# Preparing the weights of a two-layer attention block: order of loads, sums of squares, a third quantised tile

## The chip, the cores and the metric

One core of one Trainium2 chip. The metric is device time in microseconds (us): the median of three runs of the kernel before, 2736.28 (2727.44 to 2742.57). The program has five engines with queues of their own: TensorE (PE), VectorE (DVE), ScalarE (ACT), GpSimd (POOL) and SyncE (SP), which issues all the DMAs here.

## The reference

All arithmetic is fp32, x is [8, 512, 256]. Two layers, each adding two branches of the same normalised input to x:

```
xn = layernorm(x)
L0: q,k,v = split(xn @ Wq.T), split(xn @ Wk.T), split(xn @ Wv.T)   # 16 heads of 64
    k, v  = concat(mem_k, k), concat(mem_v, v)                     # 64 memory keys per head
    dots  = mix(q @ k * scale, pre_proj)                           # heads mixed: "bhij,hk->bkij"
    dots  = causal mask; keep each row's 64 largest; softmax
    out   = (mix(attn, post_proj) @ v) @ Wout.T + bout
    ffn   = fp4(silu(fp4(xn) @ fp4(w_gate).T) * (fp4(xn) @ fp4(w_up).T)) @ fp4(w_down).T
    x     = x + out + ffn
xn = layernorm(x)
L1: u = silu(xn @ Wg + bg) * (xn @ Wi + bi);  y = Cp * causal_conv(u, Bp * A^t) + Dp * u
    y = norm(y) * gamma + beta
    y = (silu(y @ Wfg + bfg) * (y @ Wfu + bfu) @ Wfd + bfd) @ Wo + bo
    lin = xn @ int4(kernel) + bias + (xn @ a) @ b
    x = x + y + lin
```

`fp4` scales blocks of 16 columns by their largest magnitude, rounds to eight levels and scales back; `int4` does it with one scale for the whole matrix, from its largest magnitude.

## The kernel before

The kernel has a preparation (to about 110 us of the profile), the attention of the eight batches (to about 2115 us), and a last stage with L0's feed-forward and L1. Only the preparation is touched; it makes from the weights what the other two need.

**Folded attention weights.** Wq, Wk and pre_proj are folded into one matrix per mixed head, `mg` (and `mgm` for the memory keys). A loop over 20 groups `j` of 16 key columns does this: PE multiplies a block-diagonal copy of Wk (`bd`, made by DVE and ACT) with Wq into a PSUM bank `pa` (8 instructions of 32 rows per group; an fp32 product leaves two records); the bank is copied to an SBUF tile `both`, by ACT for even `j` and by DVE for odd `j`; PE multiplies it with the mixing matrix `kr` into a bank `pm` (4 instructions of 256 columns); ACT copies that to `mg` or `mgm`. Groups 16 to 19 are the memory keys. Two banks serve `pa`, three `pm`, three all transposes. For a first guess at each row's 64th largest score the kernel needs the mean squares of the folded weights: after each group ACT squares `pm` into a `junk` tile (two of them, used in turn), and DVE adds up its groups of 16 (L781 and L782); at the end they are summed over `j` (L784, L785) and over partitions by a product with `ones` (L789), giving `tot`.

**L0's feed-forward weights.** `prepare` (L369 to L518) quantises w_gate and w_up in six blocks of 128 rows and 512 columns (the last has 64 rows), then w_down in two of 704 columns. A block runs through `fp4_steps` (L325): DVE takes the largest magnitudes (`w_amax`), scale and reciprocal; POOL multiplies; ACT takes `Abs` and `Sign`; six DVE steps round in `w_hi`, `w_lo` and `w_a`; POOL multiplies `w_lo` by the signs and by the scales. PE then transposes `w_lo`, and DVE or ACT copies the result from PSUM. Source, `w_a`, `w_lo` and `w_hi` have two copies, `quantise` takes them in turn.

**L1's weights** are collected in one tile, `w1s`, of 8 KB in each partition: Wfg and Wfu with gamma folded in (DVE), the int4 matrix plus a @ b (DVE, from a PSUM bank), and Wfd @ Wo (ACT). Scaling of the int4 matrix needs its largest magnitude over all partitions: DVE reduces to `mx`, POOL reduces over partitions to `mxa`, DVE computes `s` and `r` from it. When all are there, one DMA stores `w1s` to DRAM (`w1_d`). Wv, Wout and the first batch's normed tokens are transposed by PE and copied by ACT in between.

**What sets the order.** Each instruction of the preparation is recorded by `Straight` (L169) with its readers and writers, and `Plan.run` (L118) writes a fixed order for PE, ACT, DVE and POOL. It simulates: each instruction has an estimated cost (L196 to L221) and a due time, the length of what depends on it plus a lateness (`r.late`). A DMA is an SP operation of 0.5, then an operation on a shared `wire` of bytes / 240e3, then 2.0 of waiting (L252 to L259). SP's instructions are placed by the framework, not by this plan. On the chip each engine takes its instructions strictly in that order, so an instruction that waits holds all behind it. Each SP issue also waits for the DMA that used its semaphore eight issues earlier.

After the preparation, tiles of new pools take the space of its tiles, and may be written when the last reader of that space, DMAs included, is done. The first of them are the value tile `v` (ACT, L942) and `rows` (POOL, L962, a copy of the normed tokens), which PE needs for the products L975 and L1004. The pools `scr` and `x2p` (tile `xnT`) have two buffers each. Batch 0's tokens hold the first `scr` during the preparation, the next batch's tokens are loaded to the second (L883) and normed by DVE at L290 to L306, in whose queue `first_guesses` (L521), twelve or so small DVE operations around one ACT `Tanh`, six times over, stands before and after.

Of the kernel before, what the change touches and what calls it, by code (L numbers as in the profile page):

```python
# [20 lines left out]
HC = H * DH // P  # L21
MEM = 64
# [32 lines left out]
FI = 704  # L55
# [113 lines left out]
class Straight:  # L169
# [4 lines left out]

    def __init__(self, nc, pl):
        self.nc, self.pl, self.seen, self.run, self.late = nc, pl, {}, None, 0.0

# [3 lines left out]
    class Engine:  # L181
# [3 lines left out]
        def __getattr__(self, what):  # L185
            return lambda *a, **k: self.owner.call(self.name, what, a, k)

    @staticmethod
# [7 lines left out]
    @staticmethod  # L196
    def cost(eng, what, out, ins, k):
        n = 1
        for d in out.shape[1:]:
            n *= d  # L200
        wide = n
        for t in ins:
            m = 1
            for d in t.shape[1:]:
                m *= d
            if eng != "PE":
                wide = max(wide, m)
        if eng == "PE":
            if what == "transpose":
                return 0.05 + 0.0007 * n  # L210

            return (0.04 + 0.00175 * n) * (0.35 if out.shape[0] == 32 else 1.0)
        if eng == "DVE":
            if what == "tensor_tensor_scan":
                return 0.2 + 0.0021 * n
            return 0.17 if wide < 48 else 0.13 + (0.0007 if what == "tensor_scalar" else 0.00105) * wide
        if eng == "ACT":
            return 0.22 + 0.00083 * wide + {AF.Sqrt: 1.3, AF.Tanh: 1.3, AF.Silu: 0.4}.get(k.get("func"), 0.0)
        if eng == "POOL":
            return 6.0 if what == "partition_all_reduce" else 0.15 + 0.0005 * wide if what == "memset" else 0.35 + 0.0018 * wide  # L220
        return 0.5  # L221

    def call(self, name, what, a, k):
# [7 lines left out]
        func = {"func": next((t for n, t in aps if n == "func"), None)} if eng == "ACT" else {}  # L231
        cost = self.cost(eng, what, out, ins, func)
        deps = []
        for t, write in [(t, False) for t in ins] + [(t, True) for t in outs]:
# [17 lines left out]
        if what == "dma_start":  # L252
            size = 4.0
            for d in out.shape:
                size *= d
            done = self.pl.add("wire", size / 240e3, lambda: None, [op])
            done.late = self.late
            done = self.pl.add(f"wait{id(op)}", 2.0, lambda: None, [done])
            done.late = self.late  # L259
# [108 lines left out]

def prepare(nc, a, pw, scratch, ident, vt, cb, wgu_d, wd_d, w1_d, bsum_d, spare, place):  # L369

# [22 lines left out]
    for i in range(2):  # L393
        q = {"src": pw.tile([P, FI], F32, name=f"w_v{i}")}
        q["v"] = q["src"]
        for k in ("a", "lo", "hi"):
            q[k] = pw.tile([P, FI], F32, name=f"w_{k}{i}")
        for k in ("amax", "scale", "rec"):
            q[k] = pw.tile([P, FI // BLK], F32, name=f"w_{k}{i}")
        sets.append(q)  # L400

    def quantise(i, m, n, loads):
        q = {k: t[:m, : n // BLK if k in ("amax", "scale", "rec") else n] for k, t in sets[i].items()}
        for cols, src in loads:
            nc.sync.dma_start(q["src"][:, cols], src)
        for _, _, step in fp4_steps(nc, q, m, n):
            step()
        return q["lo"]

    for i, r in enumerate(range(0, FI, P)):  # L410
        m = min(P, FI - r)
        q = quantise(i % 2, m, 2 * D, [
            (slice(u * D, (u + 1) * D), a[f"L0_ffn_{n}"][r : r + m, :]) for u, n in enumerate(("w_gate", "w_up"))
        ])
# [11 lines left out]
    for o in range(DC):  # L426
        q = quantise(o, P, FI, [(slice(0, FI), a["L0_ffn_w_down"][o * P : (o + 1) * P, :])])
        for c0 in range(0, FKC, 3):
# [9 lines left out]

    w1s = pw.tile([P, 4, DC, D], F32, name="w1s")
    w1 = {i + 2: w1s[:, i] for i in range(4)}  # L440
    for i, n in enumerate(("Wg", "Wi")):
# [69 lines left out]
    for c in range(DC):  # L511
# [5 lines left out]
        nc.vector.tensor_tensor(w1[4][:, c, :], ps[:, :D], w4[:, c, :], ALU.add)  # L517
    nc.sync.dma_start(w1_d[:, 2 * DC * D :], w1s.rearrange("p i c f -> p (i c f)"))  # L518

# [81 lines left out]
def block_kernel(ctx: ExitStack, tc: tile.TileContext, a: dict, out: bass.AP):  # L601
# [48 lines left out]
    with ExitStack() as c0:  # L650
# [30 lines left out]
        with tc.tile_pool(name="prep", bufs=1) as prep, tc.tile_pool(name="prep_ps", bufs=1, space=PSUM) as pps:  # L681
            pl = Plan({})
            r = Straight(nc, pl)
            banks = [pps.tile([P, 512], F32, name=f"pps{i}") for i in range(8)]
# [23 lines left out]
            xn = scr.tile([P, NT * D], F32, name="scr").rearrange("p (t d) -> p t d", d=D)  # L708
            r.sync.dma_start(xn, x_in[0])
            por = prep.tile([P, H], F32, name="por")  # L710
            r.sync.dma_start(por, a["L0_attn_post_proj"].unsqueeze(1).to_broadcast([H, RB, H]))
# [31 lines left out]
            both = [prep.tile([P, 512], F32, name=f"both{i}") for i in range(3)]  # L743
            junk = [prep.tile([P, 512], F32, name="junk"), ring[:, 11776:]]
            sqp = prep.tile([P, NJ, DC * H], F32, name="sqp")
            for j in range(NJ):
# [33 lines left out]
                r.scalar.copy(dst, pm.rearrange("p (e k i) -> p e k i", e=DC, i=16))  # L780
                r.scalar.activation(junk[j % 2], pm, AF.Square)  # L781
                r.vector.tensor_reduce(sqp[:, j], junk[j % 2].rearrange("p (q i) -> p q i", i=16), AX.X, ALU.add)  # L782
            sq = prep.tile([P, 2, DC * H], F32, name="sq")
            r.vector.tensor_reduce(sq[:, 0], sqp[:, :16].rearrange("p j q -> p q j"), AX.X, ALU.add)  # L784
            r.vector.tensor_reduce(sq[:, 1], sqp[:, 16:].rearrange("p j q -> p q j"), AX.X, ALU.add)  # L785
            ones = prep.tile([P, P], F32, name="ones")
            r.gpsimd.memset(ones, 1.0)
            ps = bank("a")
            r.tensor.matmul(ps[:, : 2 * DC * H], ones, sq.rearrange("p i q -> p (i q)"), start=True, stop=True)  # L789
            r.vector.tensor_copy(tot.rearrange("p i e k -> p (i e k)"), ps[:, : 2 * DC * H])  # L790
# [63 lines left out]
            r.late = 0.0  # L854
            prepare(r, a, prep, lambda: bank("t"), ident, vt, cb, wgu_d, wd_d, w1_d, bsum_d, wv, ring[:, 8192 : 8192 + DC * 2 * FI])
            r.late = 1000.0
# [1034 lines left out]
```

## Time and profile before the change

| | |
|---|---|
| median of the runs | 2736.28 us |
| profiled execution, its own time | 2738.95 us |
| its span | 2737.0 us |
| preparation to PE's first L933 | 110.1 us |
| mean granted PE clock, whole span | 0.953 |
| clock 0 to 110 us | 0.89 |

The span covers the engines' work of one execution; its own time has some 2 us around it. The profile names all recorded preparation instructions by one line, the recorder's call, L239 (L248 in the changed program); they are told apart by tile. Busy time of an engine in a stretch counts its instructions' durations; a matmul of fp32 leaves two records. In a list of waits a line reads: engine and tile that waited, engine or DMA it waited for, total, number, longest. In a timeline a line's bracket is the idle time before it and the releaser.

### The profile page before, as it was taken

Reading aid. Unit: us, or ns where it says so; the run is one execution under the profiler, and the core shown is the slowest. Engines: PE = TensorE matmul, PEld = TensorE weight load, DVE = VectorE, ACT = ScalarE, POOL = GpSimd, SP = SyncE. Lnnn points to the kernel's source line nnn. Section 1 sums busy time; section 2 is a strip of 40 time slices with the busy share of each in tenths; the row PEclk is TensorE's granted clock in tenths of the full one; section 3 lists DMA queues with packets and bytes.
Section 4 is the critical chain, followed back from the end, with each engine's and each line's share of the span. In section 5 each row is a group of like instructions: output and inputs, shape, how many; then the busy total and the mean of one; then the engine's idle time right before and its main releaser. Section 6 shows DMA issues by size and latency. Waiting matters only on the chain. (4 is left out here: it accounts for less than half of the span.)

```text
span 2737.0 us, 56067 instructions
## 1 busy us (share of the span) xinstructions
PE 2516.0 (92%) x19064; PEld 1943.5 (71%) x19064; DVE 2181.5 (80%) x7022; ACT 1908.1 (70%) x5332; POOL 1058.7 (39%) x2175
## 2 busy tenths in 40 slices
PE   7899999999999999999999999999966688999997
PEld 4677877887787688778777877877755555666664
DVE  7788888798779779877987887797889688877762
ACT  4468877778797788778878977877795345544342
POOL 3203433444343434434443443344333354444330
PEclk9899999999999999999999999999988789999998
DMA  4300100100010010001000100000100021000000
GB/s 140 153 25 18 36 20 11 36 20 21 18 28 22 17 36 21 21 18 30 20 19 21 36 19 20 21 19 21 56 20 7 30 88 31 24 16 16 8 8 16
DMA packets 114859, 82.61 MB, mean 30 GB/s; under 512 B 79339, under 2 KB 108806, under 8 KB 113798
## 3 DMA queue, kind: packets, MB, share of 16 engines
q1 hardware_dynamic: 114566, 78.95, 9.6%
q8 instruction: 153, 2.51, 0.4%
q14 instruction: 140, 1.15, 0.1%
HBM read 44.04 MB, written 35.39 MB: 29 GB/s over the span
## 5 line engine op out<-in xcount | busy, mean ns | idle before, releaser
L1087 ACT ACTIVATE junk<-ring,cur 128x96 int8<-128x96 f32 (+36 forms) x1288 | 743.4, 585 | 3.7 <-POOL cur L1122 3.7
L1091 DVE TENSOR_SCALAR_CACHE_REDUCE junk<-ring,cur 128x520 int8<-128x520 f32 (+29 forms) x1208 | 574.5, 517 | 60.1 <-POOL cur L1149 58.7
L1044 PE MATMUL ps_sc<-xnT,tk 128*128 128x8 f32 (+38 forms) x2048 | 534.6, 401 | 11.9 <-ACT ring L1050 11.7
L1004 PE MATMUL ps_mi<-rows,mg 128*128 128x128 f32 x4096 | 509.1, 280 | 12.3 <-ACT scr L981 9.2
L1004 PEld LDWEIGHTS ps_mi<-rows,mg 128*128 128x128 f32 x4096 | 488.0, 194 | 43.9 <-issue 16.6
L1044 PEld LDWEIGHTS ps_sc<-xnT,tk 128*128 128x128 f32 x2048 | 338.5, 193 | 144.6 <-issue 76.5
L1186 DVE SCALAR_TENSOR_TENSOR ring<-ring,kth,e 128x520 f32<-128x520 f32 (+56 forms) x512 | 281.8, 570 | 186.2 <-ACT e L1177 181.0
L1322 PE MATMUL ps_at<-mixd,ring 128*128 128x128 f32 x2560 | 341.0, 282 | 13.3 <-POOL mixd L1279 12.5
L1322 PEld LDWEIGHTS ps_at<-mixd,ring 128*128 128x128 f32 x2560 | 314.0, 194 | 51.9 <-issue 21.3
L1157 DVE SCALAR_TENSOR_TENSOR y<-ring,cur 128x520 f32<-128x520 f32 (+56 forms) x512 | 297.5, 581 | 9.5
L1050 ACT COPY ring<-ps_sc 128x456 f32<-128x456 f32 (+56 forms) x512 | 190.4, 380 | 153.5 <-PE ps_sc L1044 151.6
L1160 DVE MAX8 top<-y 128x8 f32<-128x520 f32 (+56 forms) x512 | 255.7, 499 | 17.6
L1087 ACT ACTIVATION_READ_ACCUMULATOR junk<-ring,cur 128x1 f32 x1288 | 255.7, 198 | 0.0
L1346 PEld LDWEIGHTS ps_y<-at,v 128*64 128x64 f32 (+1 forms) x6144 | 199.3, 140 | 64.9 <-ACT at L1328 19.4
L1177 ACT ACTIVATE e<-ring 128x520 f32<-128x520 f32 (+56 forms) x512 | 229.5, 474 | 22.4 <-DVE ring L1186 21.7
L1015 ACT COPY tk<-ps_mi 128x256 f32<-128x256 f32 x512 | 172.4, 379 | 104.1 <-PE ps_mi L1004 102.1
L1103 POOL TENSOR_TENSOR cur<-base,raw 128x8 f32<-128x8 f32 x153 | 38.9, 254 | 524.6 <-ACT junk L1087 517.1
L1346 PE MATMUL ps_y<-at,v 128*64 128x64 f32 (+1 forms) x6144 | 225.0, 227 | 17.8 <-ACT at L1328 12.2
L1328 ACT COPY at<-ps_at 128x512 f32<-128x512 f32 x320 | 185.7, 583 | 74.6 <-PE ps_at L1322 73.9
L1139 POOL TENSOR_TENSOR by<-gap,minus 128x8 f32<-128x8 f32 x120 | 205.4, 1712 | 9.4
L1279 POOL TENSOR_TENSOR mixd<-mix,rden 128x512 f32<-128x512 f32 x128 | 132.4, 1054 | 105.6 <-DVE rden L1271 93.4
L239 PE MATMUL ps_gu<-mg,ring 128*128 128x352 f32 x448 | 148.9, 478 | 15.2 <-DVE hid L239 10.3
(324 smaller groups left out, 3881.7 us busy)
## 6 DMA issues: line engine op xcount, KB each, us to landing
msd<-scr SPq DMA_DIRECT2D x32, 512.0 KB
ring<-msd SPq DMA_DIRECT2D x512, 32.0 KB
scr<-in_L_attn_x_dram SPq DMA_DIRECT2D x10, 512.0 KB
mg_d<-mg SPq DMA_DIRECT2D x1, 4096.0 KB
att<-o SPq DMA_DIRECT2D x64, 64.0 KB
ring<-in_L_attn_x_dram SPq DMA_DIRECT2D x8, 512.0 KB
ring<-att SPq DMA_DIRECT2D x8, 512.0 KB
out_dram<-ring SPq DMA_DIRECT2D x8, 512.0 KB
```

Source lines behind the costliest of these rows:

```text
L1004: nc.tensor.matmul(ps[:, j * P : (j + 1) * P], mg[:, e, k + j, e2 * P : (e2 + 1) * P], toks(e), start=(e == 0), stop=(e == DC - 1),)
L1044: nc.tensor.matmul(ps[:, :ntok], q["tk"][side_of(g)][e][:, b].rearrange("p k i -> p (k i)"), o["xnT"][:, e, :ntok], start=(e == 0), stop=( ...
L1050: nc.scalar.copy(s[:, b, MEM : MEM + ntok], q.pop(("ps", b))[:, :ntok])
L1087: nc.scalar.activation(junk, src, AF.Sign, bias=thr, scale=-1.0, accum_out=raw[:, b : b + 1])
L1091: nc.vector.tensor_scalar(junk, src, thr, 0.0, ALU.is_ge, ALU.add, accum_out=raw[:, b : b + 1])
L1139: eng.tensor_tensor(by, gap[:, 1], minus, ALU.pow)
L1157: nc.vector.scalar_tensor_tensor(y, src, cur[:, 0, b : b + 1], src, ALU.is_ge, ALU.subtract, reverse1=True)
L1160: nc.vector.max(out=top[:, b, 1:], in_=y)
L1177: nc.scalar.activation(e, src, AF.Exp, scale=1.0 / SMALL)
L1186: nc.vector.scalar_tensor_tensor(src, src, kth[:, b : b + 1], e, ALU.is_ge, ALU.mult, accum_out=den[:, b : b + 1])
L1322: nc.tensor.matmul(pt[:n, b * P : (b + 1) * P], s[:, 4 * j + b, col : col + n], w["mix"][j][:, b, :], start=True, stop=True,)
L1346: nc.tensor.matmul(w["py"][j * DH : (j + 1) * DH, q * GR : (q + 1) * GR], vs[c][:n, k * DH : (k + 1) * DH], ats[c][:n, k, :], start=(c == ...
```

## The change

Six things, all in the preparation:

- The sums of squares of groups 0 to 15 are taken from the finished `mg`: after groups 7 and 15, sixteen ACT squares each, one for each head, of 2 x 128 columns read from `mg`, with an accumulator output. ACT's square of `pm` and DVE's reduction stay for groups 16 to 19 alone, with one `junk` tile.
- `w_lo` has three tiles, used in turn by all eight blocks.
- `w1s` is gone: the four matrices lie in a buffer of `x2p` (Wfg, Wfu) and one of `scr` (the int4 sum and Wfd @ Wo), stored by two DMAs.
- The plan of the preparation is `paced`: an SP operation costs at least bytes / 300e3, there is no `wire`.
- The plan's cost of `partition_all_reduce` is 2.0 instead of 6.0.
- From these, another order on all engines. On SP: the four loads of the third and fourth block (w_gate and w_up, 128 KB each) stand right after the eleven vector rows, not after ten other loads; the next batch's token load, which takes the first `scr` buffer now, stands after all stores; the two stores of L1 matrices, `bsum`'s and `mgm`'s come just before it, in the order `w1_d` from `xnT`, `wd_d`, `w1_d` from `scr`, `bsum_d`, `mgm_d`. On PE the product with `ones` is the last before L933. On DVE, `s` (from `mxa`) comes four instructions after `mx`.

```diff
@@ Straight
-    def __init__(self, nc, pl):
+    def __init__(self, nc, pl, paced=False):
...
-            return 6.0 if what == "partition_all_reduce" else ...
+            return 2.0 if what == "partition_all_reduce" else ...
...
+        if eng == "SP" and self.paced:
+            cost = max(cost, self.bytes(out) / 300e3)
...
         if what == "dma_start":
-            size = 4.0
-            for d in out.shape:
-                size *= d
-            done = self.pl.add("wire", size / 240e3, lambda: None, [op])
-            done.late = self.late
+            if not self.paced:
+                done = self.pl.add("wire", self.bytes(out) / 240e3, lambda: None, [op])
+                done.late = self.late
             done = self.pl.add(f"wait{id(op)}", 2.0, lambda: None, [done])
@@ prepare
-        for k in ("a", "lo", "hi"):
+        for k in ("a", "hi"):
             q[k] = pw.tile([P, FI], F32, name=f"w_{k}{i}")
...
+    lows = [pw.tile([P, FI], F32, name=f"w_lo{i}") for i in range(3)]
+    made = []
-    def quantise(i, m, n, loads):
-        q = {k: t[:m, : n // BLK if k in ("amax", "scale", "rec") else n] for k, t in sets[i].items()}
+    def quantise(m, n, loads):
+        i = len(made)
+        made.append(i)
+        q = {k: t[:m, : n // BLK if k in ("amax", "scale", "rec") else n] for k, t in sets[i % 2].items()}
+        q["lo"] = lows[i % 3][:m, :n]
...
-    w1s = pw.tile([P, 4, DC, D], F32, name="w1s")
-    w1 = {i + 2: w1s[:, i] for i in range(4)}
+    w1 = {}
+    for k, home in enumerate(homes):
+        for i in range(2):
+            w1[2 * k + i + 2] = home[:, i * DC * D : (i + 1) * DC * D].rearrange("p (c f) -> p c f", c=DC)
...
-    nc.sync.dma_start(w1_d[:, 2 * DC * D :], w1s.rearrange("p i c f -> p (i c f)"))
+    for k, home in enumerate(homes):
+        nc.sync.dma_start(w1_d[:, (2 * k + 2) * DC * D : (2 * k + 4) * DC * D], home)
@@ block_kernel
+            w1a = x2p.tile([P, DC, N], F32, name="xnT").rearrange("p e n -> p (e n)")
+            w1b = scr.tile([P, NT * D], F32, name="scr")
...
-            junk = [prep.tile([P, 512], F32, name="junk"), ring[:, 11776:]]
-            sqp = prep.tile([P, NJ, DC * H], F32, name="sqp")
+            junk = ring[:, 11776:]
+            sq = prep.tile([P, 2, 2, H], F32, name="sq")
+            sqp = prep.tile([P, MEM // 16, DC * H], F32, name="sqp")
+            def squares(part):
+                for k in range(H):
+                    r.scalar.activation(
+                        junk[:, : DC * P].rearrange("p (e d) -> p e d", e=DC), mg[:, :, k, part * P : (part + 1) * P],
+                        AF.Square, accum_out=sq[:, 0, part, k : k + 1],
+                    )
             for j in range(NJ):
...
-                r.scalar.activation(junk[j % 2], pm, AF.Square)
-                r.vector.tensor_reduce(sqp[:, j], junk[j % 2].rearrange("p (q i) -> p q i", i=16), AX.X, ALU.add)
-            sq = prep.tile([P, 2, DC * H], F32, name="sq")
-            r.vector.tensor_reduce(sq[:, 0], sqp[:, :16].rearrange("p j q -> p q j"), AX.X, ALU.add)
-            r.vector.tensor_reduce(sq[:, 1], sqp[:, 16:].rearrange("p j q -> p q j"), AX.X, ALU.add)
+                if j in (7, 15):
+                    squares(j // 8)
+                if j >= 16:
+                    r.scalar.activation(junk, pm, AF.Square)
+                    r.vector.tensor_reduce(sqp[:, j - 16], junk.rearrange("p (q i) -> p q i", i=16), AX.X, ALU.add)
+            r.vector.tensor_reduce(sq[:, 1].rearrange("p e k -> p (e k)"), sqp.rearrange("p j q -> p q j"), AX.X, ALU.add)
```

More of the change, by code (lines that the diff above doesn't have):

```diff
@@ L173 @@
     NAMES = {"tensor": "PE", "vector": "DVE", "scalar": "ACT", "gpsimd": "POOL", "sync": "SP"}
-    def __init__(self, nc, pl):
-        self.nc, self.pl, self.seen, self.run, self.late = nc, pl, {}, None, 0.0
+    def __init__(self, nc, pl, paced=False):
+        self.nc, self.pl, self.seen, self.run, self.late, self.paced = nc, pl, {}, None, 0.0, paced
     def __getattr__(self, name):
@@ L186, in __getattr__, with bytes @@
             return lambda *a, **k: self.owner.call(self.name, what, a, k)
+    @staticmethod
+    def bytes(t):
+        size = 4.0
+        for d in t.shape:
+            size *= d
+        return size
     @staticmethod
@@ L219, in cost @@
         if eng == "POOL":
-            return 6.0 if what == "partition_all_reduce" else 0.15 + 0.0005 * wide if what == "memset" else 0.35 + 0.0018 * wide
+            return 2.0 if what == "partition_all_reduce" else 0.15 + 0.0005 * wide if what == "memset" else 0.35 + 0.0018 * wide
         return 0.5
@@ L366, in fp4, with prepare @@
     return q["lo"]
-def prepare(nc, a, pw, scratch, ident, vt, cb, wgu_d, wd_d, w1_d, bsum_d, spare, place):
+def prepare(nc, a, pw, scratch, ident, vt, cb, wgu_d, wd_d, w1_d, bsum_d, spare, place, homes):
     def vec(n, c):
@@ L411, in prepare @@
         m = min(P, FI - r)
-        q = quantise(i % 2, m, 2 * D, [
+        q = quantise(m, 2 * D, [
             (slice(u * D, (u + 1) * D), a[f"L0_ffn_{n}"][r : r + m, :]) for u, n in enumerate(("w_gate", "w_up"))
@@ L426, in prepare @@
     for o in range(DC):
[L427 removed]
+        q = quantise(P, FI, [(slice(0, FI), a["L0_ffn_w_down"][o * P : (o + 1) * P, :])])
         for c0 in range(0, FKC, 3):
@@ L682, in block_kernel @@
             pl = Plan({})
-            r = Straight(nc, pl)
+            r = Straight(nc, pl, True)
             banks = [pps.tile([P, 512], F32, name=f"pps{i}") for i in range(8)]
@@ L788, in block_kernel @@
             ps = bank("a")
-            r.tensor.matmul(ps[:, : 2 * DC * H], ones, sq.rearrange("p i q -> p (i q)"), start=True, stop=True)
+            r.tensor.matmul(ps[:, : 2 * DC * H], ones, sq.rearrange("p i h k -> p (i h k)"), start=True, stop=True)
             r.vector.tensor_copy(tot.rearrange("p i e k -> p (i e k)"), ps[:, : 2 * DC * H])
@@ L854, in block_kernel @@
             r.late = 0.0
-            prepare(r, a, prep, lambda: bank("t"), ident, vt, cb, wgu_d, wd_d, w1_d, bsum_d, wv, ring[:, 8192 : 8192 + DC * 2 * FI])
+            prepare(r, a, prep, lambda: bank("t"), ident, vt, cb, wgu_d, wd_d, w1_d, bsum_d, wv, ring[:, 8192 : 8192 + DC * 2 * FI], (w1a, w1b))
             r.late = 1000.0
```

## The prediction

> **What bounds the kernel now.** I read in this order: busy times by stretch, the list of waits for the first 120 us, the timelines of PE, POOL, DVE and ACT there, the instruction order of both programs. First the stretches (columns: length, busy time and records of PE, weight loads, DVE, ACT, POOL; PE clock, DMA share, GB/s).
>
> ```profile
> 0.00:110.00 110.00, 83.64 (x606) 58.05 (x606) 81.20 (x174) 50.46 (x99) 41.04 (x146) 0.89 0.49 163
> 200.00:1000.00 800.00, 772.63 (x6719) 620.40 (x6718) 663.79 (x2429) 646.39 (x1938) 322.37 (x791) 0.98 0.08 23
> ```
>
> From 119.8 us on PE is the bound (772.6 of 800). In the preparation, 0 to 110 us, it is idle for 26 us. The edit's instructions all lie there; after it the built order on PE, DVE, ACT and POOL is the same, instruction by instruction. So the question is by how much PE's first long run moves. PE timeline (start, duration, ... idle before it and its releaser):
>
> ```profile
> 38.02 3.64 PE L239 MATMUL pps<-ring,bd 128*32 128x256 f32 x32 [9.22 <-DVE both L239]
> ...
> 92.52 3.75 PE L239 MATMUL pps<-ring,both 128*128 128x256 f32 x8 [5.48 <-DVE both L239]
> ...
> 110.10 2.74 PE L933 MATMUL ps_mi<-wvT,xnT 128*128 128x512 f32 x4 [0.52 <-DVE w1s L239]
> 114.59 5.39 PE L975 MATMUL ps_mi<-mgm,rows 128*128 128x512 f32 x8 [1.75 <-POOL rows L962]
> 119.82 14.45 PE L1004 MATMUL ps_mi<-rows,mg 128*128 128x128 f32 x128
> ```
>
> Two long holes, both for `both`, a PSUM copy on DVE. What held DVE: before the first hole a load (first line); in the second no wait at all, it works through 704-wide quantising steps queued ahead of the copy. The other waits:
>
> ```profile
> DVE w_amax L239 <- DMA w_v<-in_L_ffn_w_up_dram: 8.4, 4, 7.3
> ACT junk L239 <- DVE sqp L239: 8.6, 3, 5.8
> POOL rows L962 <- DMA w_d<-w1s: 15.7, 1, 15.7
> ```
>
> The last: POOL may not write the next stage's tile until the `w1s` store is finished.
>
> [...] after the 9.22 us hole 32 `bd` records take 3.64 us, elsewhere 1.93; after the 5.48 us hole 8 records of `both` take 3.75, elsewhere 1.9. [...] the 1 MB `w1s` store, issued at 110.14, flows at 410 GB/s for 2.6 us and releases ACT at 114.08, so 1.35 us lie around it. [...] POOL's 704-wide product takes 1.39 us alone and 2.60 beside DVE's chain.
>
> **The change, part by part.**
>
> *Squares.* Gone: 16 of 20 DVE reductions at 0.60 us spacing, 9.6, and a 512-wide reduction, 0.95: DVE 10.5 us less. On ACT 16 squares of 0.49 go (7.8), and 32 squares of 256 columns with an accumulator come. Their nearest rows are L1087's:
>
> ```profile
> 176.01 0.35 ACT L1087 ACTIVATE junk<-ring,cur 128x72 int8<-128x72 f32 x1
> 176.26 0.20 ACT L1087 ACTIVATION_READ_ACCUMULATOR junk<-ring,cur 128x1 f32 x1
> ```
>
> Spacing is 0.34 us at 72 columns and 0.72 at 520, so 0.00085 a column: 0.34 + 184 x 0.00085 = 0.50 (bounds 0.40 and 0.60). 32 x 0.50 = 16, ACT +8.2 on 50.5 of 110: cover is its idle time. Without that cover, five squares in a row stand ahead of an eviction, 2.5 us. Their in-order wait on DVE (8.6 us above) goes for the first sixteen.
>
> *Loads.* The second pair of weight blocks (four DMAs of 128 KB) was issued at 28.94 to 30.9 behind ten other loads; now it stands right after the vector rows, whose last issue ends at 23.1. The sources must be free: POOL must have multiplied by the signs. By DVE's new order (two reductions, four statistics, six 0.34 steps, three of 0.60, two copies) those products end at about 23.1 and 24.4. Issue then, plus the 2.3 to 2.6 us shown by the next pair (60.73 to 63.35, 63.27 to 65.59): landing at 26.2 and 27.5 instead of 32.8. DVE's copy that PE needs comes at 28.7, PE wants it at 28.9: the 9.22 us hole closes, and its slow clock (3.64 against 1.93) with it: -10.9. The loads moved past these go to 25 to 31 us; none has a reader before that.
>
> *Third `lo` tile.* Block 3 needn't wait for PE's reading of block 1. That, with 10.5 us less on DVE, lets the DVE queue reach the 704-wide work with its copies earlier: the 5.48 hole and the slow 3.75 after it go, -7.3. The tail's slow products (2.02 and 3.62 against about 1.0 and 1.9 warm) give up to -2.7. Removable: 10.9 + 7.3 + 2.7 = 21 us.
>
> *Two new waits.* (1) The partition maximum. In the new DVE order its result is wanted four instructions after its input; before, it had 15 us. Its price isn't plain:
>
> ```profile
> 51.58 0.38 POOL L239 PARTITION_ALL_REDUCE mxa<-mx  x1 [12.16 <-DVE mx L239]
> 58.69 1.62 POOL L239 TENSOR_TENSOR w_lo<-w_lo,w_v 128x512 f32<-128x512 f32 x1 [6.73 <-ACT mg L239]
> ```
>
> The record says 0.38, but POOL's next instruction, whose DVE input was done at 57.64 (ACT's long before), starts only at 58.69; the usual hop is 0.18. So 0.38 to 7.1; I take 7. Input at about 40.6 (the int4 matrix lands then, its space is free at 37 after the Wv transposes), result at 47.7. Behind DVE's wait stand an eviction copy and PE's copy of group 11; behind POOL's, the next block's product, and behind that ACT's `Abs` with squares and two `woT` evictions. PE has work from 37.2 for groups 7 to 9 (1.9 each), `bd` 10 to 12 (1.0 each) and five sets of transposes (0.5): to 48.4. ACT gets its `Abs` input at 48.9 and has 0.53 + four squares + 0.53 + one copy before the eviction that frees PE's bank, at 52: a hole of about 3.8 (at 0.38: none). (2) The POOL chain of the first w_down block. Its load is issued when POOL frees the source, at 58.4 by the same count, and takes about 3.7 (between 2.4 and the 4.4 from 75.07 to 79.48); through DVE, POOL and ACT its last DVE step ends at 72.9, then POOL's sign product 2.60 and scaling 1.92: 77.5. PE is out of other work, group 19 begun, at 75.6: 2.0.
>
> *Tail.* The squares' last sum and its product with `ones` now follow the last fold; the stores don't wait for them, L933 does: 0.5. I add 1 for a partly slow clock. 21 - 3.8 - 2.0 - 1.5 = 13.7 on PE's holes, plus the small holes of the old order (0.61, 0.72, 0.78, 0.52, 0.49, 0.52), of which about two thirds have no releaser left, 2.3: 16.
>
> *Stores and L1 homes.* The last fold was done at 110.05 and is now expected at 94. The last stores are `scr` (512 KB), then `bsum` (128 KB); the next stage's tiles wait for the latter: 640 KB at 410 GB/s, 1.55 us, plus 1.35 and 0.35 of issue, 3.25 against 3.94: another 0.7, which I keep as margin. (Bounds of this part: -1 to +1.) Homes cost no instruction: two stores for one, a 0.32 us issue on SP. SP's mg store moves before these as it did; no engine waits for it.
>
> *Load of the next batch.* `scr` being occupied, it moves from 31.7 us to the end of SP's list, behind 512 + 128 + 1024 KB of stores: 2.15 MB at 410 GB/s + 1.4 = 6.6 us after the last fold's 94, about 101. DVE's norm (L290) wants it, with the first guesses queued behind, then ACT's tanh, then ACT's evictions for PE. L290 ran at 117.04, 2.9 after POOL's release (114.14), now 97.3 + 2.9 = 100.2. A delay of 0.8, and DVE then waits 3.14 us for ACT's table load anyway: nothing.
>
> **Sum.** L975's start 114.6 becomes 98.6, gain 16. Profiled execution 2738.95 (span 2737.0 and 1.95 around it) - 16 = 2723; against the runs' median, 2736.28, 2720.
>
> **Rivals.** (1) Waits re-form. The chain of a quantised block runs DVE, POOL, ACT, DVE, POOL, PE, always in order; one late landing shifts everything by it. For it: `POOL w_v` waited 19.9 us for DVE in six pieces; my first copy has 0.2 us to spare. Against it: PE has independent groups between. If half of the 21 stays lost: 10 us, 2726. (2) The maximum costs 0.38 and PE stays warm: 16 + 3.8 = 20, 2716. Against: the 58.69 line. (3) The change doesn't do what it says: loads gated by POOL land no sooner; only DVE's 10.5 us count, and just in the second hole, 5.5: 2731. Against: POOL's sign products ended at 21.2 and 24.4 already before. (4) Slower: the late batch load alone. It takes back the gain when it lands more than 0.8 + 3.1 + 16 late, at about 119 instead of 101, that is at under 90 GB/s for 2.15 MB. Stretches with other traffic show 94 GB/s and less, but the comparable store ran at 410. At 75 GB/s: 29 + 1.4 after 94, 124, so +5: 2741.
>
> **How the numbers follow.** Forecast 0.57, rival (1) 0.20, (2) 0.12, (3) 0.06, (4) 0.05. 0.5% of the median is 13.7 us, about what a measurement of this kernel can tell from no change. Above it: 0.50 of my 0.57 and all of (2), 0.62; slower 0.05; the rest 0.33. The forecast's own range is 2716 to 2724; the runs of before spread 15 us, so three-run medians some 4 to each side. 2709 takes in (2) with that spread, 2733 (1) and (3); outside are (4) and the ends.
>
> **What would show it.** Right: no PE hole near 29 to 38, none over 4 us before 95, L975 starting at 96 to 101, L290 soon after its neighbours. In doubt: a DVE wait for `mxa` decides (2). Wrong: DVE idle before L290 by over 4 us; PE holes for `both` in new places; ACT squares over 0.6 us; a longer time with L975 early, which would mean the later stages differ.

## The result, and the profile after

The changed kernel takes 2724.23 us (median of 20 runs, 2716.57 to 2730.66), the kernel before 2735.20 (20 runs). The ratio is 0.9961, interval [0.9946, 0.9976]: 0.39% less, some 11 us. The forecast was 2720, and the range held the result. "Faster by over 0.5%", given 0.62, did not come: 0.39% lies in the case that had 0.33. Wherever a single trace is read below, its span is named beside it: 2737.0 us before, 2718.1 after.

Busy time by stretch, after (columns as in the prediction):

```profile
0.00:110.00 110.00, 85.59 (x625) 59.69 (x626) 75.60 (x168) 58.44 (x151) 40.35 (x156) 0.92 0.52 173
200.00:1000.00 800.00, 773.58 (x6829) 624.33 (x6829) 666.85 (x2442) 652.08 (x1950) 327.24 (x801) 0.99 0.08 23
```

DVE has 75.60 us of work instead of 81.20 and ACT 58.44 instead of 50.46, though the window now holds some 8 us of attention too. PE's timeline of the preparation:

```profile
30.38 1.93 PE L248 MATMUL pps<-ring,bd 128*32 128x256 f32 x32 [0.96 <-DVE both L248]
...
58.64 1.09 PE L248 MATMUL pps<-ident,w_lo 128*128 128x128 f32 x4 [9.94 <-ACT woT L248]
...
84.87 0.55 PE L248 MATMUL pps<-ident,w_lo 128*128 128x128 f32 x3 [1.15 <-POOL w_lo L248]
...
105.81 3.60 PE L1004 MATMUL ps_mi<-mgm,rows 128*128 128x512 f32 x8
...
124.20 1.88 PE L962 MATMUL ps_mi<-wvT,xnT 128*128 128x512 f32 x4
```

Both old holes are gone: the 9.22 us at 38.02 is 0.96, at a granted clock of 1.00 (1.93 for 32 `bd` records instead of 3.64 at 0.50), and nothing of the 5.48 us at 92.52 is left. A new hole of 9.94 us stands before 58.64. L975 of before, now L1004, starts at 105.81 instead of 114.59; 98.6 was predicted. The best landmark is PE's second group of value products (134.11 before, L933; 124.20 after, L962): from there the order of PE, ACT, DVE and POOL is the same in both kernels. **The preparation gained 9.9 us in these traces, where 16 were predicted.** (At the prediction's own landmark, L975, it is 8.8, and at L1004 10.6; between them the two traces differ in PE's clock and in a wait of 0.40.) I call the second group of value products *the start of the attention*.

What stands behind the new hole, in the timeline of all engines:

```profile
46.39 0.38 POOL L248 PARTITION_ALL_REDUCE mxa<-mx  x1 [5.68 <-issue]
46.80 0.15 DVE L248 TENSOR_SCALAR s<-mxa 128x1 f32<-128x1 f32 x1 [2.53 <-POOL mxa L248]
...
54.45 1.05 POOL L248 TENSOR_TENSOR w_v<-w_v,w_rec 128x512 f32<-128x512 f32 x1 [7.68 <-issue]
55.53 0.63 ACT L248 ACTIVATE w_a<-w_v 128x512 f32<-128x512 f32 x1 [10.60 <-POOL w_v L248]
...
57.93 0.57 ACT L248 COPY woT<-pps 128x512 f32<-128x512 f32 x1
...
58.64 1.09 PE L248 MATMUL pps<-ident,w_lo 128*128 128x128 f32 x4 [9.94 <-ACT woT L248]
```

POOL is done with its previous product at 40.71. The record of the reduction over partitions begins 5.68 us later and lasts 0.38; DVE has the result at once (46.80). But POOL's next product starts 7.68 us after the record, with "issue" as the releaser: nothing that the profile shows held it. Its operand `w_rec` had been ready since 44.27. ACT's `Abs` waits for this product, and behind `Abs` in ACT's queue stands the `woT` copy that PE waits for: its input has been there since PE's transposes ended at 47.70, but it starts only at 57.93, behind `Abs`, `Sign` and three squares. So POOL was held for 13.7 us, from 40.71 to 54.45, by an instruction whose record says 0.38.

### The profile page after: what moved, and what is told of

Read it like the earlier page. It is cut to its first block, busy times and chain, and to the rows that moved or that the text cites. A ratio compares the mean times of both kernels' runs of the same rounds, so it can differ in the third digit from the quotient of the medians.

```text
span 2718.1 us, 56104 instructions
## 1 busy us (share of the span) xinstructions
PE 2500.2 (92%) x19064; PEld 1934.7 (71%) x19064; DVE 2173.8 (80%) x7005; ACT 1914.2 (70%) x5380; POOL 1056.8 (39%) x2175
## 5 line engine op out<-in xcount | busy, mean ns | idle before, releaser
L1033 PE MATMUL ps_mi<-rows,mg 128*128 128x128 f32 x4096 | 507.5, 279 | 12.7 <-ACT scr L1010 9.2
L1033 PEld LDWEIGHTS ps_mi<-rows,mg 128*128 128x128 f32 x4096 | 486.6, 194 | 44.4 <-issue 15.9
L1375 PE MATMUL ps_y<-at,v 128*64 128x64 f32 (+1 forms) x6144 | 223.4, 226 | 18.3 <-ACT at L1357 12.9
```

The costliest lines, as they stand in the source:

```text
L1033: nc.tensor.matmul(ps[:, j * P : (j + 1) * P], mg[:, e, k + j, e2 * P : (e2 + 1) * P], toks(e), start=(e == 0), stop=(e == DC - 1),)
L1375: nc.tensor.matmul(w["py"][j * DH : (j + 1) * DH, q * GR : (q + 1) * GR], vs[c][:n, k * DH : (k + 1) * DH], ats[c][:n, k, :], start=(c == ...
```

## The experiments

In several runs the time did not follow the start of the attention. The table is ahead of the runs, so that each can be read against it. "Half clock" counts, of the 15 short PE holes (2.1 to 2.9 us) of the attention, those followed in the trace by a period of half PE clock; "periods" counts all periods of half PE clock from the start of the attention to the end of the trace. Experiments 5 to 8 explain both. Experiments 9 to 11 were run once, so it is their traces that are read.

| kernel | start of the attention | half clock, of 15 | periods | span of the trace | median of the runs |
|---|---|---|---|---|---|
| before | 134.11 | 15 | 67 | 2737.0 | 2735.20 (20) |
| after | 124.20 | 11 | 61 | 2718.1 | 2724.23 (20) |
| 1 maximum on PE | 114.65 | 15 | 68 | 2719.6 | 2721.70 (9) |
| 2 before, maximum on PE | 138.00 | 15 | 67 | 2741.2 | 2742.37 (20) |
| 3 tokens early | 125.28 | 13 | 62 | 2720.5 | 2723.37 (20) |
| 4 squares as before | 122.52 | 14 | 67 | 2725.1 | 2731.84 (12) |
| 9 maximum twice | 137.23 | 12 | 60 | 2729.1 | 2731.25 (1) |
| 10 order of loads alone | 122.09 | 12 | 63 | 2718.9 | 2720.86 (1) |
| 11 two `lo` tiles | 120.84 | 14 | 67 | 2722.9 | 2725.04 (1) |

### 1, 2 and 9: the reduction over partitions

Experiment 1 takes the reduction off POOL in the changed kernel, experiment 2 in the kernel before, with the same edit; experiment 9 doubles it in the changed kernel. Every such edit also makes the plan write a new order, so a run tests the edit together with its order.

```diff
-    nc.gpsimd.partition_all_reduce(mxa, mx, P, bass_isa.ReduceOp.max)
+    ps = scratch()                                    # 1 and 2
+    nc.tensor.matmul(ps[:, :P], mx.to_broadcast([P, P]), ident, start=True, stop=True)
+    nc.vector.tensor_reduce(mxa, ps[:, :P], AX.X, ALU.max)
...
+    nc.gpsimd.partition_all_reduce(mxb, mx, P, bass_isa.ReduceOp.max)     # 9
+    nc.gpsimd.partition_all_reduce(mxa, mxb, P, bass_isa.ReduceOp.max)
```

> The changed kernel, with the maximum over partitions of the int4 matrix made by PE and DVE (a product of mx, broadcast to 128 columns, with the identity, then a DVE reduction over 128 columns) instead of POOL's partition_all_reduce. Theory A: that POOL instruction holds POOL for some 13.8 us (5.7 ahead of its record, 0.4, 7.7 after it), and this makes PE's 9.94 us hole. Then the hole shrinks to under 2 us and the first L1033 products, at 109.2 in the changed kernel, start at 101 to 104. Rival B: the squares in ACT's queue ahead of the woT evictions make the hole. Then 5 us or more of it stay and L1033 starts at 107 or later.

Measured: 2721.70 us, ratio 0.9954 [0.9935, 0.9972]. Timelines of PE and POOL:

```profile
43.59 0.63 PE L248 MATMUL pps<-ident,w_lo 128*128 128x128 f32 x4 [1.02 <-ACT woT L248]
...
47.24 1.32 POOL L248 TENSOR_TENSOR w_lo<-w_lo,w_v 128x512 f32<-128x512 f32 x1 [4.93 <-DVE vt L248]
...
100.36 14.45 PE L1035 MATMUL ps_mi<-rows,mg 128*128 128x128 f32 x128
114.65 1.88 PE L964 MATMUL ps_mi<-wvT,xnT 128*128 128x512 f32 x4
```

The 9.94 us hole is 1.02, POOL waits for DVE again, L1035 (L1033 of the changed kernel) starts at 100.36, just ahead of theory A's range, and the attention 9.55 us earlier than after the change. The plan also moved the maximum itself, to 86.80 on PE, but the squares still stand in ACT's queue among the `woT` copies, so they did not make the hole. That the reduction's hold on POOL made it is shown, together with experiment 9. Only 2.5 of the 9.55 us are in the median of the runs, and the two intervals overlap.

> The kernel before, with the same replacement. Theory A: there POOL was idle from 39.4 to 51.6 and from 52 to 58.7 anyway, and the instruction's cost was hidden but for 1.05 us, so the first L1004 products, at 119.8, start at 117.5 to 120.5. Rival: it cost before what it costs after, and L1004 starts at 114 or earlier.

Measured: 2742.37, ratio 1.0022 [1.0007, 1.0037]; the products of L1006 follow at 123.71, outside both theories, and the attention starts 3.9 us later than before. Without the reduction the kernel before gains nothing, which fits that there POOL's hold lay in its idle time. The run isn't a clean test of it, since the order changed: the plan put the maximum's product at 108.77, just ahead of the last fold, and DVE keeps PE waiting 2.30 us for `w1s` instead of 0.52; the two large holes are 10.45 and 5.91 us instead of 9.22 and 5.48.

> The changed kernel with the reduction over partitions issued twice, one on the result of the other. Theory A (each issue holds POOL for all of its 5.7 before and 7.7 after the 0.38 us record): the next POOL product starts some 13 to 14 us later (at 67 to 69 instead of 54.45), PE's hole for woT grows from 9.9 to about 22 to 24, and PE's second long run of values begins at 137 to 139 instead of 124.20. Theory B (what stands before and after the record is paid once, by the first and the last of them): the product starts 0.4 to 1.5 us later, hole 10 to 11.5, second run at 124.5 to 126. Theory C (the 7.7 us are no hold, POOL waits for something else): nothing moves.

Measured, one run: 2731.25. POOL's timeline:

```profile
45.99 0.38 POOL L248 PARTITION_ALL_REDUCE mxb<-mx  x1 [5.57 <-DVE w_a L248]
53.15 1.05 POOL L248 TENSOR_TENSOR w_v<-w_v,w_rec 128x512 f32<-128x512 f32 x1 [6.78 <-issue]
60.13 0.38 POOL L248 PARTITION_ALL_REDUCE mxa<-mxb  x1 [5.93 <-issue]
...
67.52 1.25 POOL L248 TENSOR_TENSOR w_lo<-w_lo,w_v 128x512 f32<-128x512 f32 x1 [7.02 <-issue]
```

Each of the two is paid in full: 5.57 + 0.38 + 6.78 = 12.7 us for the first, and 5.93 + 0.38 + 7.02 = 13.3 us for the second, from the end of one product (54.20) to the start of the next (67.52). The attention starts at 137.23, 13.0 later than after the change, as theory A said. Where it enters was told wrong: the plan put a product between the two, the hole for `woT` stayed at 8.94 instead of 22 to 24, and two later ones came (5.42 and 4.13).

One question is open here. The change had lowered the plan's cost for this instruction from 6.0 to 2.0, away from the 13 us measured. The changed kernel with a cost of 6.0 or 13 was not run, so how much of the hole comes from this one number isn't known.

### 3, 4, 10 and 11: the parts one by one

Experiment 3 gives the second L1 home a tile of its own, so that the next batch's tokens can be loaded early again.

```diff
-            w1b = scr.tile([P, NT * D], F32, name="scr")
+            w1b = prep.tile([P, NT * D], F32, name="w1b")
```

> The changed kernel with the int4 sum and Wfd @ Wo in a tile of the preparation's own pool, so that the next batch's tokens have the second scr buffer and are loaded at some 40 us again. Theory A: DVE's wait of 3.39 us for them goes, but it was covered by ACT's table load: PE's second L962 stretch, at 124.2, starts at 123.5 to 124.5. Rival C: the late load takes back a part of the gain: 122 or earlier.

Measured: 2723.37, ratio 0.9967 [0.9955, 0.9979]. In the changed kernel DVE does wait for the tokens (its line below), here it doesn't; but the attention starts at 125.28, 1.1 later (the hole for `woT` is 11.13 here), where 123.5 to 124.5 was expected. The late load costs the kernel nothing that these runs can show.

```profile
110.12 0.43 DVE L297 BATCH_NORM_STATS2 ln_st<-scr 128x6 f32<-128x256 f32 x1 [3.39 <-DMA scr<-in_L_attn_x_dram]
```

Experiment 4 is the changed kernel with the sums of squares as before.

```diff
-                if j in (7, 15):
-                    squares(j // 8)
-                if j >= 16:
-                    r.scalar.activation(junk, pm, AF.Square)
-                    r.vector.tensor_reduce(sqp[:, j - 16], ...)
+                r.scalar.activation(junk[j % 2], pm, AF.Square)
+                r.vector.tensor_reduce(sqp[:, j], ...)
```

> The changed kernel with the sums of squares of all 20 groups taken as before (ACT squares each pm, DVE reduces); the matrices of L1 outside, loads and third tile stay. Theory A: DVE has 10.5 us more again and ACT 8 us less; the hole at the partition maximum stays, L1033 starts at 111 to 114 instead of 109.2. Rival B: without 32 squares in ACT's queue the hole goes, L1033 at 107 or earlier.

Measured: 2731.84, ratio 0.9983 [0.9968, 0.9999]. Its stretches:

```profile
0.00:110.00 110.00, 83.80 (x640) 58.93 (x641) 86.01 (x191) 51.48 (x103) 41.71 (x156) 0.95 0.52 176
```

Against the changed kernel DVE has 10.4 us more and ACT 7.0 less: the prediction's 10.5 and 8.2. Yet the attention starts 1.7 us *earlier*, at 122.52: DVE's relief was not what PE waited for while the reduction stood in the way (the hole for `woT` is 10.83 here). Nor did it close the second hole: with DVE's 10.4 us back but three `lo` tiles, PE's holes between 80 and 95 are 1.46 and 1.83 us, not 5.48. The time is 7.6 us longer all the same, which the preparation can't explain.

Experiment 10 is the kernel before with the paced plan alone. The reduction's scheduling cost, squares, tiles and homes are as before.

```diff
+        if eng == "SP" and self.paced:
+            cost = max(cost, size / 300e3)
...
-            r = Straight(nc, pl)
+            r = Straight(nc, pl, True)
```

> The kernel before with the paced plan alone (loads in order of need, the scheduling cost of the reduction, squares, tiles and homes as before). Step Loads of the prediction: the hole of 9.22 us near 29 to 38 shrinks to under 2 us, the 5.48 us hole near 87 to 92 stays (3 to 7 us), the second run of values on PE begins 8 to 12 us earlier than 134.11, at 122 to 126. Rival (the loads are gated by POOL and land no sooner): a hole of 7 to 10 us before 40, second run at 132 to 135.

Measured, one run: 2720.86. All engines' timeline:

```profile
29.33 1.93 PE L244 MATMUL pps<-ring,bd 128*32 128x256 f32 x32 [0.96 <-DVE both L244]
...
41.75 0.38 POOL L244 PARTITION_ALL_REDUCE mxa<-mx  x1 [7.35 <-DVE mx L244]
49.07 1.27 POOL L244 TENSOR_TENSOR w_lo<-w_lo,w_v 128x512 f32<-128x512 f32 x1 [6.94 <-DVE w_a L244]
...
81.32 3.75 PE L244 MATMUL pps<-ring,both 128*128 128x256 f32 x8 [4.41 <-DVE both L244]
...
122.09 1.88 PE L936 MATMUL ps_mi<-wvT,xnT 128*128 128x512 f32 x4
```

The first hole is closed, the second (4.41, and slow products after it, 3.75) is not, and the attention starts 12.0 us earlier than before: 2.1 more than the whole change gained. The same POOL hold is there, but PE has other work meanwhile: from 30 us to the second hole, which begins at 76.9, it has none of over 0.9.

Experiment 11 is the changed kernel with two `w_lo` tiles.

```diff
-    lows = [pw.tile([P, FI], F32, name=f"w_lo{i}") for i in range(3)]
+    lows = [pw.tile([P, FI], F32, name=f"w_lo{i}") for i in range(2)]
...
-        q["lo"] = lows[i % 3][:m, :n]
+        q["lo"] = lows[i % 2][:m, :n]
```

> The changed kernel with two w_lo tiles instead of three. Step Third tile of the prediction: a hole of 4 to 7 us for the copies of the late groups comes back between 80 and 95, second run of values on PE at 128 to 132 instead of 124.20. Rival (the squares and the loads alone closed that hole): no hole over 2.5 us after 70, second run at 123 to 126.

Measured, one run: 2725.04. Timelines:

```profile
41.12 0.38 POOL L248 PARTITION_ALL_REDUCE mxa<-mx  x1 [6.97 <-DVE mx L248]
48.87 2.50 POOL L248 TENSOR_TENSOR w_lo<-w_lo,w_v 128x512 f32<-128x512 f32 x2 [7.36 <-DVE both L248]
...
52.44 0.66 PE L248 MATMUL pps<-ident,w_lo 128*128 128x128 f32 x4 [1.27 <-POOL w_lo L248]
...
82.34 3.78 PE L248 MATMUL pps<-ring,both 128*128 128x256 f32 x8 [4.86 <-ACT ring L248]
...
120.84 1.88 PE L962 MATMUL ps_mi<-wvT,xnT 128*128 128x512 f32 x4
```

The hole that the third tile had closed comes back as expected (4.86, at 82.34), but the attention starts earlier, at 120.84, not at 128 to 132. With two tiles POOL takes two `w_lo` products behind the reduction, not a `w_v` product that ACT's queue hangs on, and the 9.94 us hole is 1.27. So here the third tile cost more, through the place where the plan then put the reduction, than it gave.

### 5 to 8: why the time doesn't follow the preparation

Between 200 and 1960 us PE has just 15 holes of over 2 us, 2.14 to 2.92 long, at the same places of the program in every kernel so far. One of them in two traces, PE's timeline, the kernel before and then the changed one:

```profile
403.23 2.40 PE L1044 MATMUL ps_sc<-xnT,tk 128*128 128x328 f32 x8
407.93 3.60 PE L1004 MATMUL ps_mi<-rows,mg 128*128 128x128 f32 x16 [2.30 <-ACT scr L981]
```

```profile
391.71 2.40 PE L1073 MATMUL ps_sc<-xnT,tk 128*128 128x328 f32 x8
396.41 2.05 PE L1033 MATMUL ps_mi<-rows,mg 128*128 128x128 f32 x16 [2.30 <-ACT scr L1010]
```

The hole is the same 2.30 us. After it, the same products take 3.60 in one and 2.05 in the other. Stretches of the kernel before, and then of the changed one, with the PE clock in the last column but two:

```profile
408.20:411.60 3.40, 3.40 (x18) 3.18 (x19) 2.28 (x9) 2.84 (x10) 2.35 (x7) 0.50 0.41 159
```

```profile
395.80:399.20 3.40, 2.79 (x43) 2.67 (x44) 1.93 (x7) 3.40 (x13) 2.93 (x8) 1.00 0.41 157
```

In both traces every stretch of half clock begins on one grid of 3.41 us and lasts a whole number of its periods (44 stretches before, 36 after; only the last is cut off by the end); where the grid lies against the program differs between the two. The period ahead of such a stretch need not be idle throughout: of the 15 holes in each trace, the 24 that took 60 to 86% of one period were followed by half clock in the next, and the four whose largest share of one period was 49 to 57% were not (the 2.30 us of the second trace, 49% of one period and 18% of the next, are one). The hole of 2.66 us fits no such limit: it took 43 and 35% of two periods in the first trace, 33 and 45% in the second, and half clock began both times with the second of the two. So this describes these holes and is not a rule. Where half clock followed holes of 2.49 and 2.66 us, it lasted two periods, after the others one.

What a half-clock period costs can be read from the table. Take the span less the start of the attention: 2602.8 us with 67 periods in the kernel before, 2593.9 with 61 in the changed one, 2605.0 with 68 in experiment 1. These nine traces and the five filled ones below all lie within 1.1 us of one straight line, 2500.5 us and 1.53 us for each half-clock period; my estimate of the most is 1.71, half of the 3.41 of a period. So in the traces the time follows from the start of the attention and the number of these periods, to within some 1 us. Before and after differ by 18.9 us: 9.9 from the preparation and, at 1.53 each, some 9 from six periods.

In the runs the same is seen: over the 20 runs of the changed kernel a mean clock of 0.961 goes with 2716.57 us, and 0.955 or 0.956 with the ten runs from 2725 to 2731.

The test fills the 15 holes. The products just ahead of each of the 15 are repeated, into the same bank before its eviction, so that the output is the same.

```diff
+AGAIN = {("scores", n): k for n, k in ((82, 1), (94, 3), (210, 1), (222, 3), (338, 1), (350, 3), (458, 6), (466, 1), (478, 3))}
+AGAIN |= {("queries", n): 1 for n in (80, 82, 144, 146, 208, 210)}
...
-                        for j in range(4):
+                        calls["queries"] += 1
+                        for j in [0, 1] * AGAIN.get(("queries", calls["queries"]), 0) + list(range(4)):
...
-                    for e in range(DC):
+                    calls["scores"] += 1
+                    for e in list(range(DC)) * (1 + AGAIN.get(("scores", calls["scores"]), 0)):
```

> The changed kernel, with products repeated on PE in the 15 idle stretches of 2.1 to 2.9 us that the attention has between 130 and 1960 us (same operands, same bank, before its eviction; nothing else changed). Theory A (each of these stretches costs one or two periods of 3.41 us at half PE clock, or none, by where it falls on the grid of these periods, and that makes the spread of the runs): next to no half-clock period left between 130 and 1960 us (14 were in the profile of the changed kernel), mean clock 0.967 to 0.970, time 2693 to 2702 instead of 2724, runs within 6 us of each other but for the last stages. Theory B (ACT and DVE set the pace there, the clock only fills idle time): less than 5 us gained, spread as before.

> The kernel before with the same 15 fillings. Theory A: 2702 to 2710, so that filled against filled the change is worth what its preparation gained in the traces, 9.9 us (8 to 12). Theory B (the change also acts on the later stages): the two filled kernels differ by less than 6 or by more than 14 us, or neither gains by the filling.

> The changed kernel with the maximum over partitions taken by PE and DVE, filled. It was 9.6 us earlier than the changed kernel at the start of the attention, but only 2.5 in the median of the runs. Theory A: filled it is 8 to 11 us faster than the changed kernel filled, 2683 to 2693. Theory B: again 2 to 4 us faster only.

> The changed kernel with the squares as before, filled. Its preparation was 1.7 us shorter than the changed kernel's, its runs 7.6 us longer. Theory A: filled it is 0 to 3 us faster than the changed kernel filled. Theory B: 5 to 9 us slower than it.

| filled | start of the attention | median (runs) | lowest to highest | ratio to before |
|---|---|---|---|---|
| 6 before | 134.40 | 2718.45 (17) | 2711.78 to 2723.82 | 0.9943 [0.9928, 0.9958] |
| 5 after | 122.80 | 2705.54 (4) | 2704.98 to 2706.76 | 0.9904 [0.9869, 0.9939] |
| 7 maximum on PE | 115.55 | 2699.66 (4) | 2695.34 to 2701.65 | 0.9883 [0.9848, 0.9919] |
| 8 squares as before | 122.78 | 2705.05 (5) | 2703.88 to 2711.64 | 0.9908 [0.9879, 0.9938] |

Experiment 5's stretch shows the clock:

```profile
200.00:1000.00 800.00, 781.25 (x6918) 632.13 (x6916) 665.57 (x2436) 657.39 (x1969) 325.64 (x806) 1.00 0.09 24
```

Theory A holds in kind. With more work on PE every kernel is 17 to 27 us faster by the medians, 16 to 21 by the ratios, for which the runs of before were taken beside each experiment. So ACT and DVE don't set the pace there. Experiment 8, which unfilled was 7.6 us slower than the changed kernel, is now 0.5 faster, with the attention starting at the same time; before and after differ by 12.9 us where 8 to 12 was expected, 11.6 of them at the start of the attention. The sizes were too large: 5, 6 and 7 lie 3.5 to 8.5 us above the upper ends expected. A part of this is in the traces: six half-clock periods were left in 200 to 1960 us of experiment 5 (three in 6), and 47 after 1960, which I hadn't touched. But the trace of 6 is from one of its fastest runs (2712.22), and experiment 6 still spreads over 12 us, so for its median the cause is not shown. From the start of the attention on, the traces of 5, 6, 7, 8 and 12 have 53, 49, 50, 54 and 54 half-clock periods. The advantage of the maximum on PE, 7.3 us at the start of the attention here, shows as 5.9: more than the 2.5 unfilled, less than expected, with intervals that are too wide to say whether all of it is there.

### 12: squares and third tile once the reduction is gone

The kernel before with the paced plan (10), the maximum on PE (2) and the filling (6), no other edit. Against experiment 7 it lacks the squares, the third tile and the new homes of L1's matrices.

> The kernel before with the paced order of loads and the maximum on PE and DVE, filled; squares, two w_lo tiles and w1s as before. Theory A (once the reduction is off POOL, squares and third tile are worth the 7.3 us that the prediction gave them): second run of values on PE at 121 to 125, a hole of 4 us or more near 80, time 2704 to 2711, 5 to 10 us behind the changed kernel with the maximum on PE, filled. Theory B (the order of loads and the reduction were all there was): second run at 114 to 118, time 2697 to 2702, within 3 us of it.

Measured: 2702.39 (9 runs), ratio 0.9895 [0.9867, 0.9922]. PE's timeline:

```profile
81.38 3.75 PE L244 MATMUL pps<-ring,both 128*128 128x256 f32 x8 [5.00 <-DVE both L244]
...
123.40 1.88 PE L942 MATMUL ps_mi<-wvT,xnT 128*128 128x512 f32 x4
```

The trace decides for theory A: the hole for `both` is there (5.00, with slow products after it), and the attention starts 7.9 us later than in experiment 7. The time, 2702.39, lies between the two theories, 0.4 us above B's range and 1.6 below A's; relative to the runs of before beside it (2738.27 here, 2733.03 there) it is 0.9895 against 0.9883, a difference of 3 us that the intervals don't resolve. Experiment 7, 2699.66 us, ratio 0.9883, is the fastest of all and beats both kernels.

## Why the prediction was right and wrong

**Loads.** Right. Hole of 9.22 us to 0.96, clock 1.00; alone (10) it is worth 12.0, where 10.9 were written down.

**Third `lo` tile and squares.** Right in size, on a condition that the prediction didn't name. The 5.48 us hole stays without them (10, 12), comes back without the third tile (11), and its worth with the reduction gone is 7.9 us (12 against 7, the new homes included) for the 7.3 predicted. With the reduction in place undoing either makes the attention start 1.7 (4) or 3.4 us (11) earlier. Of the two it is the third tile that the hole goes with (11 against 4); the prediction gave the credit to both. DVE -10.4 and ACT +7.0 fit; a square with accumulator is spaced 0.54 us, predicted 0.50.

**Two new waits, (1): the step that failed.** The prediction bounded the price by 0.38 and 7.1, took 7 and spent it once, as lateness of the *result*: input 40.6, result 47.7, ACT's `Abs` at 48.9, hole 3.8. The result came as said (46.80). But the 6.73 us that I read in the kernel before stood *after* the record, and delay POOL, not the result; ahead of the record there are 5.7 more. In the kernel before POOL was idle there for 12.16 us, and the record begins 0.14 after `mx` is done. The hold is 13.7 us where 7 were taken. POOL's next product came at 54.45, `Abs` at 55.53, 6.6 later than worked out. The hole is 9.94, that is 6.1 more, and 16 - 6.1 = 9.9 is what the start of the attention gained; that it agrees to the tenth is luck, since other landmarks give 8.8 and 10.6 and smaller terms were off too. Experiment 1, without the reduction, gains 19.5; the prediction's sum without it is 16 + 3.8 = 19.8. Rival (2), which gave that gain at 2716, asked for a maximum that costs 0.38. The wait that was to decide it, DVE's for `mxa`, was 2.53 us: it ends with the result and says nothing of the 7.7 us that POOL is held after it.

**(2), the w_down chain:** 1.15 for 2.0. (The prediction compares POOL's 704-wide product at 2.60 with one of another kind at 1.39; the sign product itself takes 2.60 at 90.70 and 1.67 at 95.25 in the kernel before, so the difference is smaller than it looks there, and that DVE makes it was not shown.) **Tail:** PE waits 1.51 for DVE's `sq` and 0.41 for `tot`, and the four products of L962 behind them run at a granted clock of 0.55, 3.57 for 1.88: 3.6 us, where 1.5 was allowed. **Stores:** the last fold was done at 100.5, not 94 (the same 6 us), and POOL's `rows` came at 103.78, 3.3 after it; 3.25 predicted. (The 3.94 set against it counts from the store's issue; from the fold's end it was 4.0.) **Load of the next batch:** DVE waited 3.39, not 0.8. The prediction's sum of stores leaves out the 768 KB `wd_d` store, issued at 98.57, and took 410 GB/s; from there to 109.70 the DMAs moved 274 on average. The table load's cover held: PE lost 0.40, and undoing it (3) gave nothing. Rival (4) was far off its point of decision.

**From the preparation to the time.** The prediction took a microsecond at L975 for one at the end. That holds over many runs only roughly: 9.9 in the traces' preparation, 11.0 in the medians, but 9.6 against 2.5 in experiment 1, and the wrong sign in 4. Shown is that the half-clock periods carry the difference between the traces (the line through the counts of the table) and most of what 4 lost in its runs (experiment 8 beside 4). Why experiments 1 and 4 met them in so many of their runs isn't settled; that their preparations leave PE at another place of the grid was not tried by itself. So it is in part luck that the range held the time: it was wide enough for rivals (1) to (3) as well, and the runs of the changed kernel alone spread over 14 us.

## What to carry to other kernels

Price an instruction by what its engine can do next, not by its record: look for idle time with "issue" as the releaser on *both* sides of it (5.68 and 7.68 us around the 0.38 here), and ask what is queued behind. A relief elsewhere can move such an instruction from idle time onto the path, so judge the parts of a change by undoing each. Where PE is the bound, as in the attention here, short holes can cost more than their length (those of 2.1 to 2.9 us did, by 1.53 us for each half-clock period after them), and filling them is worth a try. A difference of a few microseconds is to be judged by a landmark in the trace together with the granted clock, not by the time alone.

## What the runs showed of the hardware

A reduction over partitions held POOL for 12.7 to 13.7 us from the end of one product to the start of the next: 13.7 in the changed kernel, 12.7 and 13.3 for the two of experiment 9. The record shows 0.38 of it; 5.6 to 5.9 lie before the record and 6.8 to 7.7 after it, and a second reduction a single product later pays again. Where POOL had long been idle when `mx` came, the record begins 0.13 to 0.14 us after `mx` is done (at 51.58 in the kernel before, 41.75 in experiment 10, 41.12 in 11), and 6.73, 6.94 and 7.36 us pass from its end to the next product. What fills the times around the record the traces don't show.

A PE hole of 2.14 or 2.15 us, well under the 3.41 us of a period, was followed by a period at half clock where it took 60 to 63% of one period (clock 0.50 from 626.61 to 630.02 us of the kernel before, for one), and was not where it took 57% (at 1095.34 us of the changed kernel). From the start of the attention on, a half-clock period cost 1.53 us by the line through 14 traces.
